# Two attentions in turn on one core: one more place for a piece before each first turn of maxima, and one load moved from a piece's place to the side of a unit

## The chip, the core and the metric

The kernel runs on one core of one Trainium2 chip. The time is the device time of one execution in microseconds (us), and lower is better. A core has a matrix engine (TensorE, PE in the profile; its weight loads are listed as PEld), a vector engine (VectorE, DVE), a scalar engine (ScalarE, ACT), a general engine (GpSimd, POOL) and an engine that only issues transfers (SyncE, SP). Each engine works through its own queue of instructions in order; they wait for one another through semaphores. Matrix products land in PSUM, which has eight banks of 128 partitions x 512 float32; the other engines read them from there. TensorE's clock can be cut; the profile gives the granted share.

## What is computed

Four batch elements of 1024 tokens with 256 channels go through two layers, each an attention and a feed-forward part, every one with a residual and a LayerNorm behind it:

```python
x = _layernorm(x + _L0_attn_ref(x, ...))  # 16 heads of 16; q and k normalised, rotated; softmax over all 1024 keys
x = _layernorm(x + _L0_ffn_ref(x, ...))   # silu(x Wg) * (x Wu), then Wd; hidden size 768
x = _layernorm(x + _L1_attn_ref(x, ...))  # 8 heads of 32, causal, with a geometric term in the scores
x = _layernorm(x + _L1_ffn_ref(x, ...))   # 16 experts, two per token, 12 of them MLPs of 1024
```

The change concerns the order of work around the second attention of each element (causal), which is in short

```python
scores = q @ k.T * scale, masked above the diagonal, + head_scales * geo
attn = softmax(scores)
out = (attn @ v) @ w_out
```

and the loading of the first attention's queries and keys of element 2.

## The kernel before

**Order by hand.** The program writes out the order of every engine's instructions itself (no scheduler moves them). The long stages are Python generators that emit a *unit* of attention work and then `yield`; `weave` (L1182) runs such a generator and emits *pieces* of other work between its units: projections, transposes and feed-forward parts of the same or the neighbouring element. After unit u of n it brings the number of emitted pieces up to `total * (u + 1) // n`. So the pieces are spread evenly over the units. Before the pieces of a unit, `tick()` emits the small steps that were booked for this point with `later(k, ...)` (k units later), and one entry of `side` is emitted from unit `side_at` on. Entries of `mid` are counted as pieces: from unit `at` on each takes the place of a unit's pieces.

**The stages.** First attentions and second attentions alternate: `first_units(1)`, then `second_units(0)` with element 1's pieces, then `first_units(2)`, `second_units(1)` and so on. The last second attention, `second_units(3)`, is run by a loop of its own with a plan of 29 entries.

**The first attention** (`first_units`, L1089, 64 units per element). A unit has four heads' scores (L491, `sc`), the maxima products of a coming group (L467, `mx`), the exponentials on ScalarE (L500, `pe`), the maxima on VectorE (L470) and the product with the values (L509, `av`). `load_heads(b, pr)` issues two transfers on SP (L379 and L380, `ss` and `xr`) and books eight small POOL steps (L386), one in each of the next eight ticks.

**The second attention** (`second_units(b)`, L1142, 29 units). Its first work is to find each row's maximum: `Maxima1.unit(t, u)` makes one block of scores for four heads (L972, `mx`, four banks), and VectorE reduces each bank (L982 with the mask on the diagonal, L986 without). There are 24 such blocks in four sets: (half 0, group 0) with four, (half 0, group 1) with four, and two sets of eight for half 1. After the last block of a set, `split` (L993 to L997) writes the maxima as three bfloat16 parts into `nm`, five small steps on VectorE in half 0. In the next unit, `turn` (L1002, `ptm`) transposes them on TensorE, and VectorE copies the result to `nmT` (L1005). The scores for the softmax (L1022, `sc`) take `nmT` as a second product, so that the maxima come off within PSUM; then exponentials (L1033), the mask on POOL (L1036), the product with the values and the sums (L1059, `av` and `dn`), and the division in four steps (L1077 on VectorE, L1079 on POOL).

How many blocks of maxima a unit has is written in `many`: one in units 0 to 3, two in unit 4, one in 5 to 8, two in 9 to 11, one in 12 to 19, none in the last nine. Scores begin when fewer than 19 blocks are left, that is in unit 5. So units 0 to 4 have only maxima. The first set ends in unit 3, and its turn is the first thing in unit 4.

**The pieces beside it.** For `second_units(0)` and `second_units(1)` there are 28: the nine of `first_end(b)`, numbered 0 to 8 here, are two transposes of the first attention's output (`pta`, L613), the last unload (`pto`, L524, L527, L528), two projections (`ppa`, L598, each with the residual and the LayerNorm's moments of two row tiles on VectorE, L553 to L556), two more `pta` and two more `ppa`; from 9 on come the first 19 of `ffn0(b)`: a transpose (`ptx`, L647), gate-and-up pieces (`gu`, L665, L675 to L678) and `down` pieces (`dn`, L683, each with a residual). For `second_units(2)` there are 45 pieces: the same nine and all 36 of `ffn0(3)`.

**Banks.** `ps_s` has six banks, given out in turn; a new user waits until the one six before it has been read. The blocks of maxima, the scores, `ptm` and all pieces in the second attentions take theirs from it. In the first attentions the pieces use the single bank of `ps_m`.

**The load in question.** In the weave of `first_units(1)`, `load_heads(2, 0)` is an entry of `mid` with `at` 30. The pieces there are 65: four of `project_v(1)`, nine of `first_end(0)`, 36 of `ffn0(0)` and 16 of `project1(0)`; numbers 30 and 31 are the two `down` pieces of the second quarter of `ffn0(0)`.

Of the kernel before, what the change touches and what calls it, by code (L numbers as in the profile page):

```python
# [20 lines left out]
B, S, C = 4, 1024, 256  # L21
# [14 lines left out]
def postln_layers_kernel(ctx: ExitStack, tc: tile.TileContext, a: dict, out: bass.AP):  # L36
# [75 lines left out]
    with ExitStack() as main:  # L112
# [27 lines left out]
        def bank(name, big):  # L140

            if big:
                return ps_s.tile([P, 512], F32, tag="s", name=name)
            return ps_m.tile([P, 512], F32, tag="m", name=name)
# [14 lines left out]
        def take_xin(b, j, name):  # L159
            key, t = xin_here.pop(0)  # L160
            assert key == (b, j, name)
            if xin_next and not xin_here:
                load_ahead()
            return t
# [127 lines left out]
        def project_v(b):  # L292
            def piece(j, big):
                xin = take_xin(b, j, "v") if b else xin0[j]
                ps = bank(f"v0_{b}_{j}", big)
                for i in range(2):
                    for c in range(2):
                        nc.tensor.matmul(
                            ps[:, i * 256 : (i + 1) * 256],
                            xin[:, c, i * P : (i + 1) * P],  # L300
                            w0[:, c, 512:768],
                            start=c == 0,
                            stop=c == 1,
                        )
                if b and xin_next:
                    load_ahead()
                nc.scalar.copy(va0[:, 2 * j : 2 * j + 2, :, 0:D0], ps.rearrange("p (t h d) -> p t h d", t=2, h=H0))

            return [lambda big, j=j: piece(j, big) for j in range(4)]
# [779 lines left out]
        def first_units(b):  # L1089

            oq0[b] = act.tile([P, TB, C], F32, tag="oq", bufs=2, name=f"oq0_{b}")
            last = None
            for g in range(G0):
                n = 4 * b + g
                at = Attend(groups[n], oq0[b])
                for i in range(16):

                    k, j = divmod(16 * n + i + LEAD, 16)
                    mx = groups.get(k)
                    for hp in range(2):  # L1100

                        then = []
                        for h in range(2):
                            if mx is not None:
                                then += [at.head(i, 2 * hp + h), mx.head(j, 2 * (1 - hp) + h)]
                            elif hp == 0:
                                then += [at.head(i, 2 * h), at.head(i, 2 * h + 1)]
                        for fn in then:
                            fn()
                        if hp == 0:  # L1110
                            if i > 0:
                                at.values(i - 1)
                            elif last is not None:
                                last.values(15)
                            if j == 3:
                                groups[k - 1].turn(0, 1, name="a")
                            if i == 5 and last is not None:
                                last.unload(1)
                            if j == 10 and mx is not None:
                                mx.turn(0, 0, name="a")  # L1120
                            if i == 11:
                                at.unload(0)
                            if j >= 12 and k + 1 in groups:
                                groups[k + 1].turn((j - 12) // 2, j % 2)
                    if j == 0:
                        groups[k - 1].close(1)
                    if j == 3 and k + 1 < G0 * B:
                        groups[k + 1] = Maxima(*divmod(k + 1, G0))
                    if j >= 4 and k + 1 in groups:
                        groups[k + 1].rotate(4)  # L1130
                    if j == 8 and mx is not None:
                        mx.close(0)
                    yield
                last = at
            last.values(15)

            def end(big):
                last.unload(1, big)

            ends[b] = end  # L1140

        def second_units(b):  # L1142


            oT1[b] = act.tile([P, G1, S], F32, tag="oq", bufs=2, name=f"oT1_{b}")
            mx = [Maxima1(b, g) for g in range(G1)]
            at = [Attend1(m, oT1[b]) for m in mx]
            halves = ([(t, 0) for t in range(4)], [(t, u) for t in range(4, TB) for u in range(2)])
            blocks = [(h, g) for h in range(2) for g in range(G1)]
            ahead = [(h, g, k) for h, g in blocks for k in range(len(halves[h]))]  # L1150
            scores = [(g, i) for h, g in blocks for i in ((0, 1, 2, 3) if h == 0 else range(4, 12))]
            many = [1] * 4 + [2] + [1] * 4 + [2] * 3 + [1] * 8 + [0] * 9
            last, to_turn = None, []
            for n in many:
                sc = scores.pop(0) if len(ahead) < 19 else None
                turns, to_turn = to_turn, []
                todo = [ahead.pop(0) for _ in range(n)]

                def maxima():
                    h, g, k = todo.pop(0)  # L1160
                    mx[g].unit(*halves[h][k])
                    if k == len(halves[h]) - 1:
                        mx[g].split(h)
                        to_turn.append((g, h))

                if sc is not None:
                    g, i = sc
                    at[g].scores(i)
                    if len(todo) > 1:
                        maxima()  # L1170
                if last is not None:
                    at[last[0]].values(last[1])
                last = sc
                for g, h in turns:
                    mx[g].turn(h)
                while todo:
                    maxima()
                yield
            assert not scores
            at[last[0]].values(last[1])  # L1180

        def weave(units, n, pieces, big, mid=(), at=0, side=(), side_at=0, rate=1):  # L1182


            mid, side = list(mid), list(side)
            done, total = 0, len(pieces) + len(mid)
            for u, _ in enumerate(units):
                tick()
                for _ in range(rate if u >= side_at else 0):
                    if side:  # L1190
                        side.pop(0)()
                if u >= at and mid:
                    mid.pop(0)(big)
                    done += 1
                    continue
                left = len(pieces)
                while left and (done < total * (u + 1) // n):
                    pieces.pop(0)(big)
                    done, left = done + 1, left - 1
            for piece in pieces:  # L1200
                piece(big)
                tick()
            for step in side:
                step()
                tick()
# [136 lines left out]
        def first_end(b):  # L1342

            out = out_project0(b)
            return out[:2] + [lambda big: ends[b](big)] + out[2:]
# [14 lines left out]
        load_heads(1, 1)  # L1360
        for t in range(TB):
            load_x(1, t)
        weave(first_units(1), 64, project_v(1) + first_end(0) + ffn0(0) + project1(0), False, [lambda big: load_heads(2, 0)], 30)
        for b in (1, 2):
            ffn = ffn0(b)
            weave(
                second_units(b - 1),
                29,
                first_end(b) + ffn[:cut],
                True,  # L1370
                side=load_v(b + 1) + [lambda b=b: load_heads(b + 1, 1)],
            )
            weave(
                first_units(b + 1),
                64,
                second_end(b - 1, ffn[cut:]) + project1(b),
                False,
                [lambda big, b=b: load_heads(b + 2, 0)] if b + 2 < B else (),
                30,
                dispatch(b - 1, False),  # L1380
                26,
            )
# [16 lines left out]
        nc.sync.dma_start(b1.rearrange("p e f -> p (e f)"), a["b1"])  # L1399
        b2 = mw.tile([P, EM, C], F32, name="b2")  # L1400
        nc.sync.dma_start(b2.rearrange("p e c -> p (e c)"), a["b2"].partition_broadcast(P))
        weave(second_units(2), 29, first_end(3) + ffn0(3), True)
        out2, (tu2, lo2) = out_project1(2), route(2)
        proj, out3, (tu, lo) = project1(3), out_project1(3), route(3)
        straight(proj[:4] + out2[:1] + proj[4:8] + out2[1:2])
# [350 lines left out]
```

## Time and profile before

| | |
|---|---|
| median of the runs | 2390.05 us (3 runs: 2387.06, 2390.05, 2404.72) |
| the profiled execution | 2392.53 us, of it the span from the first to the last instruction 2390.8 us |
| TensorE's granted clock, mean | 0.966 |
| first attention of element 1 (`first_units(1)`) | ends at about 693 us |
| first turns of the second attentions (L1002) | 705.56, 1173.38, 1629.55 and 1835.50 us |
| TensorE idle before them | 3.53, 3.05, 3.24 and 3.36 us |

A line of the profile's timeline gives the start, the duration, the engine, the line of the program, the operation, the tiles as out<-in, the shapes and the number of instructions merged; in square brackets stands the idle time of that engine before it and what ended it. A float32 product is two matmul instructions. A line of the waits gives who waited for whom, the total in us, the number of times and the longest. A window's line gives for each engine the busy time and the number of instructions. A busy TensorE isn't always at its peak: matmuls that wait for a bank between two others of the same line can be merged into one busy row.

### The profile page before, as it was taken

The page shows a single profiled execution, that of the slowest core. Times are in us where ns is not written, and L with a number is a line of the kernel's source. Part 1 is how long each engine was busy: PE and PEld are TensorE (multiplying, and loading weights), DVE is VectorE, ACT ScalarE, POOL GpSimd, SP SyncE. Part 2 cuts the span into 40 slices and gives each one's busy share as a digit, 9 for nine tenths or more (in the row PEclk, how much of TensorE's full clock was granted, in tenths as well). Part 3 has the DMA queues.
Part 4 walks back from the last instruction along what each step waited for, and adds up shares of the span by engine and source line. Part 5 has one row for each costly group of instructions (what it writes and reads, how often), then busy time and mean ns, then how long its engine had stood idle before and what let it go on. Part 6 is the DMA issues. An engine that isn't in the chain of part 4 may idle for free.

```text
span 2390.8 us, 36349 instructions
## 1 busy us (share of the span) xinstructions
PE 2287.3 (96%) x14004; PEld 1122.2 (47%) x14004; DVE 1384.3 (58%) x3259; ACT 1030.9 (43%) x2063; POOL 761.9 (32%) x1181
## 2 busy tenths in 40 slices
PE   8999999999999999999999999999999994999986
PEld 5333334444444444334444434345556443666654
DVE  7666666666557567776674767726645785111124
ACT  2665655554542355555324565562332331222222
POOL 5326337052105121553241321111112154222235
PEclk9999999999999999999899999998999986999998
DMA  4143121000000000000100000012000012444463
GB/s 112 52 149 117 60 75 35 1 28 1 1 28 1 1 1 1 28 28 28 55 1 1 1 1 8 31 34 103 1 1 1 1 55 71 107 122 108 107 181 95
DMA packets 81662, 109.63 MB, mean 46 GB/s; under 512 B 9040, under 2 KB 71248, under 8 KB 79824
## 3 DMA queue, kind: packets, MB, share of 16 engines
q1 hardware_dynamic: 52208, 73.87, 9.4%
q0 software_dynamic: 10176, 16.39, 3.4%
q10 hardware_dynamic: 19104, 17.04, 2.3%
q8 instruction: 110, 1.80, 0.3%
q14 instruction: 64, 0.52, 0.1%
HBM read 67.86 MB, written 39.42 MB: 45 GB/s over the span
## 4 chain that ended last, share of the span: by engine, by line
PE 86%; DVE 8%; DMA 2%; issue 1%; ACT 1%; POOL 1%; SPq 0%; DVEq 0%; POOLq 0%; ACTq 0%
PE sc L491 21%; PE av L509 10%; PE gu L665 7%; PE ph L1619 6%; PE py L1655 6%; PE mx L972 5%; PE sc L1022 4%; PE p L941 4%; PE dn L683 3%; PE av L1059 3%; PE ppa L598 3%; PE dn L1059 2%; PE mx L467 2%; DVE masked L982 2%; PE qk L321 2%; PE pt L458 1%
## 5 line engine op out<-in xcount | busy, mean ns | idle before, releaser
L470 DVE TENSOR_REDUCE part<-mx 128x1 f32<-128x512 f32 x1024 | 657.0, 684 | 311.1 <-PE mx L467 307.3
L500 ACT ACTIVATE pe<-sc 128x512 f32<-128x512 f32 x1024 | 554.7, 596 | 415.0 <-PE mx L467 388.0
L467 PE MATMUL mx<-kT,qT 32*128 32x512 f32 x2048 | 604.3, 639 | 0.6 <-DVE part L470 0.2
L491 PE MATMUL sc<-qT,kT 32*128 32x512 f32 x2048 | 586.2, 639 | 0.4 <-ACT pe L500 0.4
L509 PE MATMUL av<-pe,va 128*32 128x512 f32 x2048 | 273.0, 605 | 0.0
L491 PEld LDWEIGHTS sc<-qT,kT 32*128 32x128 f32 x2048 | 164.9, 183 | 212.4 <-issue 173.0
L1033 ACT ACTIVATE pe<-sc 128x512 f32<-128x512 f32 (+3 forms) x384 | 157.2, 497 | 203.5 <-PE sc L1022 203.4
L982 DVE CUSTOM_DVE_ANT_0 masked<-mx,mask_w 128x128 bf16<-128x128 f32 (+3 forms) x256 | 125.6, 491 | 111.6 <-PE mx L972 82.5
L1655 PE MATMUL py<-f,hTm 128*128 128x256 f32 x768 | 175.1, 387 | 14.6 <-DVE yo L1657 14.6
L467 PEld LDWEIGHTS mx<-kT,qT 32*128 32x128 f32 x2048 | 173.6, 183 | 18.7 <-DVE part L470 10.8
L1619 PE MATMUL ph<-dmT,f 128*128 128x512 f32 x384 | 168.6, 597 | 0.0
L1655 PEld LDWEIGHTS py<-f,hTm 128*128 128x128 f32 x768 | 148.5, 195 | 41.2 <-DVE yo L1657 15.4
L1657 DVE TENSOR_TENSOR yo<-py,b 128x256 f32<-128x256 f32 x48 | 20.3, 423 | 245.2 <-PE py L1655 245.2
L1036 POOL TENSOR_SCALAR_AFFINE_SELECT pe<-pe 128x256 f32<-128x256 f32 x128 | 52.0, 415 | 292.0 <-ACT pe L1033 290.4
L972 PE MATMUL mx<-kT,qT 32*128 32x512 f32 (+3 forms) x768 | 136.5, 569 | 3.6 <-DVE x L553 2.8
L386 POOL TENSOR_TENSOR ss<-ss,neg_half 128x16 f32<-128x16 f32 x48 | 139.1, 2911 | 0.6
L1663 POOL DMA_INDIRECT acc_d<-yo,dm x40 | 62.6, 1565 | 228.5 <-DVE yo L1660 180.2
L509 PEld LDWEIGHTS av<-pe,va 128*32 128x32 f32 x2048 | 40.4, 108 | 192.6 <-issue 188.7
L1022 PE MATMUL sc<-qT,kT 32*128 32x512 f32 (+3 forms) x768 | 122.7, 563 | 3.9 <-DVE part L982 1.6
L1627 ACT ACTIVATE hTm<-ph,b 128x512 f32<-128x512 f32 x96 | 60.7, 683 | 144.2 <-PE ph L1619 144.2
L1619 PEld LDWEIGHTS ph<-dmT,f 128*128 128x128 f32 x384 | 73.5, 192 | 88.0 <-issue 86.5
L665 PE MATMUL gu<-xTf,wg 128*128 128x256 f32 x384 | 110.2, 410 | 3.8 <-DVE hT L678 3.3
(370 smaller groups left out, 3013.1 us busy)
## 6 DMA issues: line engine op xcount, KB each, us to landing
f<-in_fc SPq DMA_DIRECT2D x14, 1024.0 KB, 4.9
f<-in_fc ACTq DMA_DIRECT2D x10, 1024.0 KB, 5.8
disp_d<-empty ACTq DMA_DIRECT2D x12, 520.0 KB, 3.4
xink<-in_xT SPq DMA_DIRECT2D x24, 256.0 KB, 3.0
qk_d<-xs SPq DMA_DIRECT2D x6, 1024.0 KB, 5.1
xr<-qk_d SPq DMA_DIRECT2D x6, 1024.0 KB, 5.9
dm<-disp_d SPq DMA_DIRECT2D x11, 520.0 KB, 5.7
x<-in_x SPq DMA_DIRECT2D x32, 128.0 KB, 2.5
```

Of the source, the lines that this page charges most:

```text
L467: nc.tensor.matmul(sc, self.qT[r, t * P : (t + 1) * P], self.kT[r, u * 512 : (u + 1) * 512], start=True, stop=True)
L470: return lambda: nc.vector.tensor_reduce(self.part[:, t, u, h : h + 1], sc, AX.X, ALU.max, negate=True)
L491: nc.tensor.matmul(sc, self.m.kT[r, kt * P : (kt + 1) * P], self.m.qT[r, qb * 512 : (qb + 1) * 512], start=True, stop=True)
L500: nc.scalar.activation(self.pes[i, h // 2][:, h % 2, :], sc, AF.Exp)
L509: nc.tensor.matmul(self.av[32 * h : 32 * h + 32, :], va0[:, kt, 4 * self.g + h, :], self.pes[i, h // 2][:, h % 2, :], start=kt == 0, stop= ...
L665: nc.tensor.matmul(ps[:, i * 256 : (i + 1) * 256], (wg, wu)[i][:, c, f * P : (f + 1) * P], xT[j][:, c, :], start=c == 0, stop=c == 1,)
L972: nc.tensor.matmul(scs[h][:, :n], qT[r, t * P : (t + 1) * P], kT[r, u * 512 : u * 512 + n], start=True, stop=True,)
L982: nc.vector.tensor_tensor_reduce(masked[:, :n], scs[h][:, :n], mask_w[:, 512 - n :], -1.0, -NEG, ALU.add, ALU.min, part)
L1022: nc.tensor.matmul(scs[h][:, off:], ones_h[r, :] if w else kT[r, kt * P : (kt + 1) * P], (self.m.nmT if w else qT)[r, q], start=w == 0, st ...
L1033: nc.scalar.activation(pe[:, j, off:], scs[2 * hp + j][:, off:], AF.Exp)
L1619: nc.tensor.matmul(ph[:, i * CAP : (i + 1) * CAP], f1[:, c, (f + i) * P : (f + i + 1) * P], dmT[:, c, :], start=c == 0, stop=c == 1,)
L1655: nc.tensor.matmul(py[:, :C], hT[:, f, c * P : (c + 1) * P], f2[:, f, :], start=f == 0, stop=f == FF1 // P - 1)
```

## The change

Two edits. In `second_units`, one more `yield` is put ahead of a turn, where a set of maxima has just been split, no scores have begun, and the element isn't the last. That is so once per element, in unit 4, for the elements 0, 1 and 2. At this `yield` the weave runs a tick, a side step if there is one, and the pieces that are due; the three weaves count 30 places instead of 29. In the weave of `first_units(1)`, `load_heads(2, 0)` goes from `mid` to `side`, from the same unit 30 on: it no longer counts as a piece and no longer takes the place of one.

```diff
@@ second_units
                         mx[g].split(h)
                         to_turn.append((g, h))
 
+                if turns and sc is None and b < B - 1:
+
+                    yield
                 if sc is not None:
                     g, i = sc
                     at[g].scores(i)
@@ the weaves
-        weave(first_units(1), 64, project_v(1) + first_end(0) + ffn0(0) + project1(0), False, [lambda big: load_heads(2, 0)], 30)
+        weave(
+            first_units(1),
+            64,
+            project_v(1) + first_end(0) + ffn0(0) + project1(0),
+            False,
+            side=[lambda: load_heads(2, 0)],
+            side_at=30,
+        )
         for b in (1, 2):
             ffn = ffn0(b)
             weave(
                 second_units(b - 1),
-                29,
+                30,
                 first_end(b) + ffn[:cut],
...
-        weave(second_units(2), 29, first_end(3) + ffn0(3), True)
+        weave(second_units(2), 30, first_end(3) + ffn0(3), True)
```

## The prediction

> **What bounds the kernel now.** I read the page's busy times first, then the waits, then the timeline and the table of stretches around the two edited places. All times are of the profiled execution: span 2390.8 us, 2392.53 us by the clock of the runs, so 1.7 us lie outside the span. That is 2.5 us above the median of 2390.05; 1% of the median is 23.9 us, which is about what a measurement of this kernel can tell from no change.
>
> ```profile
> PE 2287.3 (96%) x14004; PEld 1122.2 (47%) x14004; DVE 1384.3 (58%) x3259; ACT 1030.9 (43%) x2063; POOL 761.9 (32%) x1181
> PE 86%; DVE 8%; DMA 2%; issue 1%; ACT 1%; POOL 1%; SPq 0%; DVEq 0%; POOLq 0%; ACTq 0%
> ```
>
> TensorE (PE) carries 86% of the chain that ended last; VectorE (DVE) carries 8%. So a change of order can only win where PE stands idle, is held by a full buffer, or runs at a lower clock. The waits say where an earlier piece could help:
>
> ```profile
> PEld L1002 <- DVE nm L995: 25.2, 15, 3.8
> PE ptm L1002 <- DVE nm L995: 18.0, 11, 3.5
> ```
>
> L1002 turns the split maxima. It waits for L995, the last step of the split: 18.0 us of PE idle time over 11 waits, the longest 3.5. Four of these are the first turns of the four second attentions (3.53, 3.05, 3.24 and 3.36 us). The change touches the first three of them. The first, in time:
>
> ```profile
> 703.66 0.69 DVE L982 CUSTOM_DVE_ANT_0 masked<-mx,mask_w 128x512 bf16<-128x512 f32 x1
> ...
> 705.30 0.20 DVE L995 CAST nm<-part 128x16 bf16<-128x16 f32 x1
> ...
> 705.56 0.61 PE L1002 MATMUL ptm<-ident_h,nm 128*128 128x128 bf16 x4 [3.53 <-DVE nm L995]
> 706.10 2.85 PE L972 MATMUL mx<-kT,qT 32*128 32x128 f32 x16
> 708.88 3.78 PE L598 MATMUL ppa<-w0p,oTa 128*128 128x256 f32 x8
> 712.59 1.96 PE L1022 MATMUL sc<-qT,kT 32*128 32x512 f32 x8
> ```
>
> PE ends `pto` at 702.0 and waits; DVE works through four maxima and five small split steps without a gap. Then comes the first projection `ppa`, in 3.78 us; the next, at 716.83, takes 1.99. The table of stretches says why (columns: stretch, length, busy and count per engine, granted clock, DMA share and GB/s):
>
> ```profile
> 702.00:706.00 4.00, 0.47 (x5) 0.35 (x4) 3.50 (x13) 0.00 (x0) 0.00 (x0) 0.76 0.83 310
> 706.00:713.00 7.00, 7.00 (x30) 4.96 (x32) 3.76 (x19) 0.00 (x0) 0.00 (x0) 0.50 0.01 2
> 1170.00:1174.00 4.00, 0.95 (x10) 0.42 (x8) 3.42 (x13) 0.00 (x0) 0.00 (x0) 0.50 0.93 314
> 1630.00:1647.00 17.00, 17.00 (x62) 10.88 (x64) 10.14 (x41) 2.65 (x5) 1.74 (x4) 0.53 0.19 81
> ```
>
> After the wait PE has half its clock: for 7 us in the first attention, most of 17 in the third. In the second it has half of it already in the wait. The other edited place is element 1's first attention:
>
> ```profile
> 514.32 2.86 PE L683 MATMUL dn<-wd,hT 128*128 128x256 f32 x12
> 517.70 2.86 PE L683 MATMUL dn<-wd,hT 128*128 128x256 f32 x12 [0.52 <-DVE x L553]
> ```
>
> Two `down` pieces stand back to back, and the second waits for the one `ps_m` bank that the first filled.
>
> **The change part by part.**
>
> *Loading beside a unit.* As `mid`, the load took unit 30's place, so unit 30 had no piece and unit 31 two. As `side`, it issues the same two DMAs on SP and books the same eight POOL steps at the same tick; 65 pieces over 64 units then give one each until the last unit. Nothing on SP or POOL moves; the transfer has landed 5 us after issue and its cover (33 units) is unchanged. What goes is the 0.52 us wait, and the stretched first half of unit 31: its eight matmuls last from 510.27 to 512.25, where an unhindered half (513.25 to 514.32) takes 1.07; a weight load in it waited 0.71 for ACT. 1.98 - 1.07 + 0.52 = **1.4 us off**. At least the 0.5 goes.
>
> *The extra place, first and second attention.* 28 pieces over 30 places instead of 29: pieces 3 to 12 each come one unit earlier, unit 14 has none, and from unit 15 on all is as before. Piece 3, the first `ppa`, falls into the wait: 2.0 us at full clock in a 3.5 us hole. But its residual (two adds, two statistics, two aggregates: 712.70 to 714.79 on DVE, 2.06 us) now stands ahead of `nmT` and the next eight maxima on DVE, the busy engine here. PE's next eight matmul groups need banks that these free: the two of t=1 wait for the residual and for `nmT` (to 708.6), then for two maxima at 0.44. I get the next `ppa` at about 710.0 where one starts now at 708.88: 1.1 later. At half clock it ends 3.75 later, 713.8 against 712.59 now: 1.2 behind, with a 1.93 us piece more done: **0.8 off**; at full clock 2.6 off. In the second attention the same sum gives **0.9**. I take half clock for both, because the stretch from the turn to 707.4 has little work for PE.
>
> *The pieces one unit earlier.* Units 9 to 11 have two maxima each and DVE is nearly full there. `ppa` number four with its 2.06 us residual leaves unit 9 for unit 8, which has one; gate-and-up pieces (0.85 us on DVE) come in. DVE then starts unit 10's maxima about 1.9 us earlier (744.57 now). From 748.4 to 760.2 unit 11 takes 11.8 us, with the clock at half from 751.8 to 758.7. Were that dip gone, I count 8.9 us. Between 0.5 and 3.4, I take **2.0 for each of the two attentions**: near the DVE figure, since the dip is not sure to go. Unit 14 without a piece: a unit's 4.7 us of own matmuls hide 2.1 us of exponentials, so nothing; if that cover fails, 0.9, as in unit 31 above. The loads of the next heads issue at the same point of SP's queue; their POOL steps come one unit earlier, while POOL is idle (53 us before 716.0).
>
> *The third attention.* 45 pieces over 30. Into the hole comes only a `pta` (0.66 us); the two `ppa` that now run at half clock from 1640.25 to 1646.86 come a unit earlier, at 1633.6, back to back. That is PE's densest work, and in all three attentions the clock came back after such a stretch (ends 714.3, 1181.9, 1646.1). I expect it back near 1639, the next scores at 1644.1 instead of 1646.79, and 0.6 of work done ahead: **3.3 off**; at least 1, at most 4.5.
>
> Sum: 1.4 + 0.8 + 0.9 + 2 x 2.0 + 3.3 = 10.4; 2392.5 - 10.4 = 2382. By the lower ends it is 0.5 + 0 + 0 + 2 x 0.5 + 1 = 2.5 (2390); by the upper ends 1.4 + 2 x 2.6 + 2 x 3.4 + 4.5 = 17.9 (2374.6).
>
> **The rivals.**
>
> *The vector engine gives it all back* (slower). The chain from 698 to 705 is DVE's, and what is put ahead of its next maxima pushes them by 2.06 us. If the first scores follow DVE's last maximum instead of PE's `ppa`, each of three attentions pays the 2.06 and unit 14 its 0.9: 3 x 2.96 - 1.4 = 7.5, so 2400. It decides where PE is done before DVE; against it, DVE idles 1.82 us before the first residual today, so PE ends last by that much. In the third attention the piece has no residual, which weakens it again.
>
> *The gap was no loss.* The pieces fill it, the waits return at the banks, and only the edit on the load is won: -1.4, 2391. For it: both engines do the same work in the stretch, and DVE binds until 710.9.
>
> *The clock is held.* If the filled gap keeps the clock up, the 10.2, 17.1 and 17.1 us at half speed (from 704.0, 1164.8 and 1629.1) are in question. In them PE works without a long wait for 8.2 us (from 706.1), 8.5 (from 1173.4) and 11.4 (from 1634.7), 28 in all, of which full clock would save half; 2 of that are in the 3.3 already. So up to 12 beyond the forecast: 2370. Against it: in the second attention the clock fell at 1164.8, more than 5 us before the wait, in a stretch with no idle gap of TensorE. The Trainium skill ("TensorE: Matmul & The Clock Gate", HAM oscillation) would have it that idle gaps over some 3 us drop the clock to half and that shorter ones don't; by it, all three holes cut below 3 us would give this rival. The trace agrees with the half (0.50), but 1164.8 shows a fall without such a gap.
>
> *It doesn't do what it says.* The condition holds once per attention (unit 4: 20 tiles left, the split just made), and the places are then 30 in all three, as the callers say; I give this nothing.
>
> **How the numbers follow.** Forecast (5 to 17 off): 0.62, at **2382**. No loss in the gap: 0.18. Clock held: 0.10. Slower by DVE: 0.10. The range takes in the forecast's bounds, the 3 us that the lowest run lies under the median, and the no-loss rival: 2371 to 2395. It leaves out part of the slower and of the clock rival. None of the cases reaches 1% of 2390 by its own price (2366 or 2414), so: faster by over 1% 0.03, within 1% 0.95, slower by over 1% 0.02.
>
> **What would show it.** Right: `ptm`'s first wait falls from 3.5 to about 1.5 us in two attentions and by 0.6 in the third; `ppa` stands ahead of it; the 0.52 between the two `dn` is gone; unit 10's maxima start earlier against unit 9's; the third attention's half clock ends some 7 us sooner. Wrong: DVE ending the wait ahead of the first scores; a new idle gap at unit 14; a half-clock stretch longer than before. The sum is off if the clock falls or returns one window sooner or later: it decides most of the 2.0s and the 3.3.

## The result and the profile after

The changed kernel takes 2381.73 us (median of 17 runs, 2376.80 to 2386.51) where the kernel before takes 2390.05 (17 runs, 2385.08 to 2404.72). The ratio is 0.9955, with a 95% interval from 0.9942 to 0.9967; the two medians alone are 8.3 us apart (0.9965). The forecast was 2382, faster by less than 1%.

The profiled execution of after has a span of 2384.8 us. The chain and the waits that answer to those of before:

```profile
PE 85%; DVE 9%; DMA 2%; issue 1%; ACT 1%; POOL 1%; SPq 0%; DVEq 0%; POOLq 0%; ACTq 0%
```

```profile
PEld L1002 <- DVE nm L995: 21.7, 14, 3.6
PE ptm L1002 <- DVE nm L995: 14.6, 11, 3.4
```

TensorE waits 3.4 us less in sum for the split (18.0 before). That is far less than the 8.3 us won, so the shorter waits alone don't account for the result. The timeline of after around the first turn of the first second attention, with TensorE's rows and one of VectorE:

```profile
704.19 0.66 PE L524 MATMUL pto<-ident,avs 128*128 128x128 f32 x4
704.69 1.89 PE L598 MATMUL ppa<-w0p,oTa 128*128 128x256 f32 x8
...
708.42 0.40 PE L1002 MATMUL ptm<-ident_h,nm 128*128 128x128 bf16 x4 [1.84 <-DVE nm L995]
...
708.87 0.41 DVE L553 TENSOR_TENSOR x<-ppa,x 128x256 f32<-128x256 f32 x1
...
710.33 2.85 PE L972 MATMUL mx<-kT,qT 32*128 32x256 f32 x8 [0.46 <-DVE x L553]
...
713.11 3.23 PE L598 MATMUL ppa<-w0p,oTa 128*128 128x256 f32 x8
...
716.26 1.14 PE L1022 MATMUL sc<-qT,kT 32*128 32x512 f32 x8
```

The first `ppa` stands in the wait and takes 1.89 us; 1.84 us of waiting are left. Its residual is ahead of the next maxima on VectorE, and the products of the second block wait for it (0.46 us). The second `ppa` takes 3.23 us, partly at half clock. From the turn to the first scores it is 7.84 us, where it was 7.03: longer, as forecast, with one projection more done.

The clock is where the two profiles differ most. TensorE's granted clock in the second attentions of elements 0 to 3 (columns: stretch, length, busy time and count of PE, PEld, DVE, ACT and POOL, granted clock, DMA share and GB/s), first before, then after:

```profile
693.68:853.06 159.38, 151.49 (x1092) 76.20 (x1089) 92.80 (x269) 53.67 (x126) 46.39 (x63) 0.94 0.04 11
1160.57:1320.77 160.20, 152.80 (x1092) 76.80 (x1088) 92.81 (x269) 53.77 (x126) 47.06 (x64) 0.91 0.06 17
1615.53:1816.95 201.42, 193.94 (x1313) 115.53 (x1309) 114.51 (x324) 62.38 (x149) 29.74 (x70) 0.96 0.09 31
1816.95:2017.98 201.03, 161.97 (x1102) 85.07 (x1101) 145.21 (x485) 55.37 (x130) 72.28 (x155) 0.83 0.10 33
```

```profile
696.50:850.02 153.52, 147.25 (x1093) 74.98 (x1089) 91.96 (x269) 53.90 (x126) 46.63 (x63) 0.98 0.04 12
1157.58:1314.09 156.51, 149.58 (x1093) 74.83 (x1089) 92.13 (x269) 54.00 (x126) 47.29 (x64) 0.97 0.06 18
1608.90:1805.74 196.84, 187.52 (x1312) 111.35 (x1309) 114.15 (x324) 62.64 (x149) 29.88 (x70) 0.98 0.09 32
1805.74:2011.97 206.23, 167.57 (x1101) 87.22 (x1100) 145.24 (x485) 55.50 (x130) 72.17 (x155) 0.81 0.09 32
```

The three changed attentions take 506.9 us instead of 521.0, and the clock in them is 0.97 to 0.98 instead of 0.91 to 0.96. By the trace's record of the clock they stand at half clock for 23.9 us instead of 64.9. This pair is the widest apart: two later traces with these units as before give 514.4 and 515.2 us, four with them as in the change 507.2 to 509.8. The fourth, whose code is the same, took 5 us longer, at 0.81 instead of 0.83; and the first attention of element 0, also the same, 296.1 instead of 292.4. So one pair of profiles differs by several us in places that the change doesn't touch, and the experiments had to be read by stages and by the clock.

### The profile page after: what moved, and what is told of

It reads as the page before. It is cut to its first block, busy times and chain, and to the rows that moved or that the text cites. A ratio compares the mean times of both kernels' runs of the same rounds, so it can differ in the third digit from the quotient of the medians.

```text
span 2384.8 us, 36347 instructions
## 1 busy us (share of the span) xinstructions
PE 2281.3 (96%) x14004; PEld 1117.3 (47%) x14004; DVE 1381.8 (58%) x3259; ACT 1033.2 (43%) x2063; POOL 763.5 (32%) x1181
## 4 chain that ended last, share of the span: by engine, by line
PE 85%; DVE 9%; DMA 2%; issue 1%; ACT 1%; POOL 1%; SPq 0%; DVEq 0%; POOLq 0%; ACTq 0%
PE sc L491 21%; PE av L509 10%; PE gu L665 7%; PE ph L1629 6%; PE py L1665 6%; PE mx L972 4%; PE sc L1022 4%; PE p L941 4%; PE dn L683 3%; PE av L1059 3%; PE ppa L598 2%; PE mx L467 2%; PE dn L1059 2%; DVE masked L982 2%; PE qk L321 2%; PE pt L458 1%
```

## The experiments

All runs but those of the result were made in three groups, each on one chip and beside the kernel before. Two quantities are worked out for each: the sum of the three changed second attentions in its profiled execution, with the time at half clock in it, and, from all its runs, the half-clock time of the whole execution, 2 x (1 - granted clock) x span. The ratios are those on record; they are near the quotients of the medians, but not the same.

| kernel | median us (runs) | ratio to before, 95% interval | half clock, mean us | attentions 0 to 2: us / of it at half clock |
|---|---|---|---|---|
| before, by group | 2389.4 (35), 2393.0 (35), 2393.8 (28) | | 153, 162, 162 | 521.0 / 64.9 |
| before, again | 2396.2 (12) | 1.0004 (0.9985 to 1.0023) | 164 | 514.4 / 47.8 |
| the change; again | 2381.7 (17); 2383.9 (11) | 0.9955 (0.9942 to 0.9967); 0.9949 (0.9932 to 0.9965) | 127; 131 | 506.9 / 23.9; 507.2 / 23.9 |
| load edit only | 2390.3 (12) | 1.0003 (0.9981 to 1.0025) | 162 | 515.2 / 51.2 |
| extra place only | 2382.3 (12) | 0.9972 (0.9956 to 0.9987) | 127 | 509.0 / 37.5 |
| place behind the turn | 2388.0 (12) | 0.9984 (0.9967 to 1.0000) | 141 | 517.4 / 47.8 |
| hole behind unit 4 | 2387.9 (12) | 1.0001 (0.9978 to 1.0023) | 151 | 521.8 / 61.4 |
| hole behind unit 5 | 2387.3 (12) | 0.9971 (0.9954 to 0.9987) | 146 | 508.2 / 34.1 |
| unread products in the wait | 2390.3 (12) | 0.9982 (0.9951 to 1.0012) | 139 | 508.9 / 27.3 |
| hole behind unit 4, filled with unread products | 2401.4 (12) | 1.0016 (0.9992 to 1.0040) | 155 | 520.4 / 47.8 |
| the change and unread products | 2384.0 (12) | 0.9950 (0.9926 to 0.9973) | 121 | 511.5 / 27.3 |
| a place in the fourth too; again | 2379.4 (12); 2379.4 (6) | 0.9941 (0.9917 to 0.9965); 0.9938 (0.9915 to 0.9961) | 127; 124 | 507.6 / 34.1; 509.8 / 34.1 |

**The two edits apart.** The first kernel has the load as `side` and everything else as before; the second has the extra place, and the load as `mid`.

```diff
# load edit only, against before
-        weave(first_units(1), 64, ..., False, [lambda big: load_heads(2, 0)], 30)
+        weave(first_units(1), 64, ..., False, side=[lambda: load_heads(2, 0)], side_at=30)
# extra place only, against the change
-            side=[lambda: load_heads(2, 0)],
-            side_at=30,
+            [lambda big: load_heads(2, 0)], 30
```

> Edit on the load alone, second attentions as before. My theory: 1.4 us off, all of it in units 30 to 32 of element 1's first attention (18.4 us instead of 19.8), so about 2388.6 against 2390; the first turns' waits stay at 3.0 to 3.5 us. Rival (the load was most of the win): 5 us or more off.

> The extra place alone, the load as before. My theory: about 7 us off (8.3 less 1.4), 2383; units 30 to 32 of element 1's first attention take 19.8 us again; first waits 1.8, 1.8 and 2.8 us as in the changed kernel. Rival (the load was most of the win): 3 us off or less.

From the start of unit 30 to that of unit 33, element 1's first attention takes 19.80 us in the traces with `mid` and 18.36 in all with `side`. So the load edit is worth 1.44 us; its runs can't show so little (0.9981 to 1.0025). The extra place alone has 0.9972, and the two intervals overlap with that of the change: the place is nearly all of the win. The rival that the load was most of it is out. One expectation missed: the first two waits with the extra place alone are 0.91 and 0.00 us in its trace instead of 1.8. The projections in them ran for the most part at half clock and took 2.57 and 3.03 us, where the changed kernel's took 1.89.

**The wait filled, or the pieces earlier?** One kernel moves the extra place behind the turn: all pieces come as early as in the change, only the wait stays empty. The other leaves unit 4 without a piece: the first projection stands in the wait and every other piece where it stood before.

```diff
# place behind the turn, against the change
-                if turns and sc is None and b < B - 1:
-                    yield
...
                 for g, h in turns:
                     mx[g].turn(h)
+                if turns and last is None and b < B - 1:
+                    yield
# hole behind unit 4, against the change (extra=4; the weaves count 29)
-                while left and (done < total * (u + 1) // n):
+                while left and (done < total * (u + 1 - (u > extra)) // n):
```

> Both edits, but the extra place stands behind the turn instead of ahead of it: the pieces come as early in the later units as in the change, the waits aren't filled. Theory A (filling the wait is what pays in units 3 to 6, about 1.9 us in each of two attentions, and the earlier pieces about 3 us more in units 9 to 15): waits of 3.0 to 3.5 us stay, about 3 us of the 8.3 are lost, 2385. Theory B (the earlier pieces alone pay): 2382, same as the change within 2 us. Theory C (the filled wait alone pays): 2388 or more.

> Both edits, but the place behind unit 4 stays empty, so that only the piece in the wait comes earlier and all others stand where they stood before. Theory A: waits of 1.8, 1.8 and 2.8 us, units 9 to 15 as long as before, about 4 us of the 8.3 lost, 2386. Theory B (the earlier pieces alone pay): 2388 or more. Theory C (the filled wait alone pays): 2382.

Neither half won what the change wins. The runs with the place behind the turn lie at 0.9984, on the edge of the load edit's own 0.9994; those with the hole at 1.0001. The intervals are wide and leave room for theory A, whose 2385 and 2386 are a ratio of about 0.998. The traces say more. The three attentions take 161.1, 158.4 and 197.9 us with the place behind the turn, and 160.6, 159.8 and 201.4 us with the hole; in three traces with these units as before they take 157.4 to 159.4, 154.1 to 160.2 and 201.2 to 201.4. So the filled wait alone won nothing in its trace, and the earlier pieces alone won only in the third attention.

The third attention is the clearest place. Two projections that stand behind the first scores in the kernel before stand ahead of them in the change. Before, then after:

```profile
1640.25 6.61 PE L598 MATMUL ppa<-w0p,oTa 128*128 128x256 f32 x16
1646.79 0.93 PE L1022 MATMUL sc<-qT,kT 32*128 32x384 f32 x8
```

```profile
1627.64 5.07 PE L598 MATMUL ppa<-w0p,oTa 128*128 128x256 f32 x16
1632.64 1.14 PE L1022 MATMUL sc<-qT,kT 32*128 32x512 f32 x8
```

In all eight traces that have the pair ahead of the first scores this attention takes 196.7 to 198.3 us, with 6.8 to 10.2 of it at half clock, also where its wait isn't filled. In five of the six that have the pair behind them it takes 201.2 to 202.5 us, with 13.7 to 17.1 at half clock. The sixth, with unread products in the wait (below), takes 198.9 us with 6.8.

In the first attention the hole's trace shows how the filled wait is given back. The first scores start 3.99 us after the turn instead of 7.03, yet units 5 and 6 then take 20.5 us instead of 14.9:

```profile
706.91 0.40 PE L1002 MATMUL ptm<-ident_h,nm 128*128 128x128 bf16 x4 [0.73 <-DVE nm L995]
...
710.90 2.81 PE L1022 MATMUL sc<-qT,kT 32*128 32x512 f32 x6
...
717.38 3.78 PE L598 MATMUL ppa<-w0p,oTa 128*128 128x256 f32 x8
...
721.10 1.40 PE L1022 MATMUL sc<-qT,kT 32*128 32x384 f32 x8
```

```profile
707.00:711.90 4.90, 3.84 (x24) 2.40 (x24) 4.13 (x18) 0.00 (x0) 3.23 (x3) 1.00 0.04 17
711.90:722.10 10.20, 10.17 (x35) 6.33 (x36) 5.06 (x18) 2.06 (x4) 3.68 (x3) 0.50 0.00 0
```

The scores stretch to 2.8 us: their weight loads wait three times for maxima that VectorE has not read yet (0.15, 0.15 and 0.28 us), and while TensorE does so little, the clock falls to half for three windows of 3.4 us. The next projection runs at half clock again. That is the slower rival's place, though not its price: VectorE's maxima come last there.

**Is it the clock?** Unread products keep TensorE busy and move nothing. In the first kernel six of them stand in the wait of the kernel before; in the second four fill the hole of the last experiment; in the third three follow the piece in the changed kernel's wait.

```diff
+        def spin(name, n):
+            w = ps_m.tile([P, 512], F32, tag="m", name=f"spin_{name}")
+            for _ in range(n):
+                nc.tensor.matmul(w[:, 0:256], ones, wd[:, 0, :], start=True, stop=True)
# in the wait: 6 in the kernel before, 3 in the changed one; in the hole: 4, at the end of unit 4
+                if turns and sc is None and b < B - 1:
+                    spin(f"w{b}", 6)
                 for g, h in turns:
                     mx[g].turn(h)
```

> The kernel before, with six products whose result nobody reads (2.9 us at full clock) put ahead of the first turn in elements 0 to 2: TensorE works through the wait, no piece moves and VectorE gets nothing. Theory K (what pays is that the clock is at half for less time): the clock falls one or two windows of 3.4 us later but still falls, since the stretch behind the turn has little work; it is back after the first projection as before, so 3 to 10 us less at half clock per attention, 0.4 us of time for each: 4 to 8 us off, 2382 to 2386. Theory P (moving useful work into the wait is what pays): no gain, 2389 to 2391.

> The kernel with the piece in the wait and an empty place behind unit 4, with four such unread products (1.9 us at full clock) in that empty place. Theory K: the empty place cost the clock; dense products there bring it back by the time of the first scores or one window later, the half-clock stretches fall from about 10 to 7 us, and the time falls from 2388 to 2384 or 2385, though 2 us of idle products per attention are added. Theory P: the products only cost, 2390 to 2394.

> The change, with three unread products (1.4 us at full clock) behind the piece in the wait, ahead of the first turn of elements 0 to 2. Theory K: the clock still falls in the stretch behind the turn; 0 to 3 us off, 2379 to 2382. Theory P: nothing, 2382, since what is left of the wait (1.8, 1.8 and 2.8 us) covers them.

In the first one's trace these are the same units as in the prediction's first timeline, with no piece moved:

```profile
701.98 2.75 PE L1145 MATMUL spin_w<-wd,ones 128*128 128x256 f32 x12
705.67 0.40 PE L1002 MATMUL ptm<-ident_h,nm 128*128 128x128 bf16 x4 [0.94 <-DVE nm L995]
706.00 2.01 PE L972 MATMUL mx<-kT,qT 32*128 32x128 f32 x16
707.94 1.99 PE L598 MATMUL ppa<-w0p,oTa 128*128 128x256 f32 x8
709.87 1.19 PE L1022 MATMUL sc<-qT,kT 32*128 32x512 f32 x8
```

The turn comes no earlier (705.67 against 705.56), but the `ppa` behind it takes 1.99 us instead of 3.78, and the scores start 2.7 us sooner, because the clock stayed up through these units. In that execution the three attentions took 508.9 us, almost as little as with the change. So in one execution keeping the clock was enough to win as much. The runs don't show that it is so each time. They fall into two groups of six, 2378.5 to 2383.1 us at a granted clock of 0.973 to 0.977 and 2397.4 to 2399.4 at 0.965 to 0.967, with none near the median; the traced execution is of the first. What the slow six lost is not on record, and it need not be in the changed units: the fourth second attention takes 201.0 to 207.1 us in nine of the twelve traces that have it unchanged, and 214.2 to 215.2 in three.

The second kernel missed both expectations: half clock in the three attentions fell from 61.4 to 47.8 us, as theory K had it, but their time only from 521.8 to 520.4, and the runs show no gain (1.0016). Its trace is also one of the three with a long fourth attention (214.2 us), so its median isn't the price of the products alone. The third won nothing on the change: 0.9950.

**The dense piece behind unit 4.** The empty place is moved one unit on: the first projection in the wait, the second behind unit 4, none behind unit 5, the rest as before (`extra=5`).

> Both edits, with the empty place behind unit 5: the first projection stands in the wait and the second behind unit 4, all later pieces where they stood before. Empty place behind unit 4: 2388, nothing won; empty place behind unit 14: the change, 2382. Theory K (a dense piece behind unit 4 brings the clock back, and the later units matter only through their own dips): units 3 to 6 as in the change, units 9 to 15 as before; the second attentions 0 to 2 take about 512 us together, between 518 before and 507 to 509 with the change: 2384 to 2386. Theory L (the shift in units 9 to 15 is what pays): 2388 or more.

Up to the turn of unit 7 this kernel has done the same pieces as the one with the hole behind unit 4, and as the kernel before. Those units of the first attention take 37.4 us with the hole behind unit 4, 33.8 to 34.6 in three traces of before's order, and 31.0 here. (Five traces of the change's order take 31.8 to 35.5 us for them, with a transpose of 0.66 us more done, so one trace of each kernel is thin evidence.) In this trace the clock was at half from 698.6 to 705.4, nearly as in the other one (698.2 to 705.0), so the two came to the turn alike; then:

```profile
706.36 0.40 PE L1002 MATMUL ptm<-ident_h,nm 128*128 128x128 bf16 x4
...
710.53 1.99 PE L598 MATMUL ppa<-w0p,oTa 128*128 128x256 f32 x8
712.46 1.19 PE L1022 MATMUL sc<-qT,kT 32*128 32x512 f32 x8
```

With a projection at 710.5 the clock stays up until 749.8; with nothing there it fell at 711.9 for 10.2 us. The three attentions take 508.2 us, close to the change's 507. By this trace theory L is out for the attentions themselves. The time, 2387.3, lies between the two ends and above the expected 2386; its interval overlaps with the change's, and its fourth attention was long in the trace (215.0 us). Whether the shift of the later pieces is worth the rest is not settled.

**The change and the kernel before once more.**

> The change once more, on the chip of the others: 2380 to 2384; the second attentions 0 to 2 take 505 to 511 us together, at 20 to 40 us of half clock.

> The kernel before, for another trace: the second attentions 0 to 2 take 514 to 522 us together, at 50 to 65 us of half clock, where the change's take 505 to 511 at 20 to 40. If they take less than 512, the two traces of before in hand were unlucky ones.

The change came as expected. The kernel before took 2396.2 us, the three attentions within their range at 514.4 us, but with 47.8 us at half clock where at least 50 were expected. The fourth attention of this trace of before took 215.2 us, that of the other 201.0, with the same program:

```profile
1810.22:2025.43 215.21, 175.39 (x1102) 90.05 (x1101) 145.14 (x485) 55.38 (x130) 71.47 (x155) 0.76 0.09 31
```

**A place in the fourth attention too.** The condition `b < B - 1` is dropped, and one of unit 4's two projection pieces in the hand-written plan goes to the new place.

```diff
-                if turns and sc is None and b < B - 1:
+                if turns and sc is None:
...
+        plan.insert(4, [plan[4].pop(0)])
         for u, _ in enumerate(second_units(3)):
```

> The change, with an extra place ahead of the first turn in the fourth second attention too: one projection piece of unit 4's two (2.0 us, no VectorE work) goes into its wait of 3.36 us. All theories: the wait there falls to about 1.4 us; 1.5 to 3 us off against the change, 2379 to 2380. If it gives nothing, the bank or VectorE's maxima were what unit 4 waited for.

> The change with a place ahead of the fourth first turn as well, beside the change itself: 2 to 3 us less than the change (wait of 3.4 us to about 1.4), 2378 to 2380.

In the second of these groups the six runs lie from 2374.4 to 2379.8 and the change's eleven from 2379.2 to 2387.9; the medians differ by 4.5 us. The fourth attention's first turn:

```profile
1818.21 1.99 PE L941 MATMUL p<-xTa,w1q 128*128 128x256 f32 x8 [0.29 <-ACT xTa L648]
1821.28 0.40 PE L1002 MATMUL ptm<-ident_h,nm 128*128 128x128 bf16 x4 [1.07 <-DVE nm L995]
...
1823.54 3.66 PE L941 MATMUL p<-xTa,w1k 128*128 128x256 f32 x8
```

The wait of 3.36 us is down to 1.07, and the piece there needs nothing of VectorE. This version beats both kernels: 2379.4 in two groups, 0.994 of before. Its fourth attention takes 198.3 and 196.3 us where the change's two traces have 206.2 and 207.1, which is more than the wait gave; the time at half clock in it is 64.6 and 61.0 us instead of 77.8 and 78.5. That the place caused this too is not shown.

## Why the prediction was right, and where its steps were off

The sum was 10.4 us off, from 2392.5 to 2382; measured were 8.3 by the medians of the same group. That the time itself was met to 0.3 us is partly luck: the sum was taken off a profiled execution that lay 2.5 us above the median, and off the median it would have given about 2380. By stages, with the three traces in which these units run as in the kernel before (the load edit's among them) and the five in which they run as in the change (the extra place alone and the two with a place in the fourth attention among them), the extra place gave 516.9 - 508.1 = 8.8 us in the attentions, where the terms came to 9.0.

- **The load.** 1.4 forecast, 1.44 measured, in the place named.
- **The waits.** Forecast about 1.5, 1.5 and 0.6 less in the third; measured 1.84, 1.80 and 2.80 (0.44 less). The scores after the first turn were to start later with one projection more done: 7.84 us behind the turn against 7.03, as forecast.
- **The first, second and third attention.** Forecast 2.8, 2.9 and 3.3. Measured, as means over those traces: 4.1 (158.6 to 154.5), 0.4 (157.0 to 156.6) and 4.3 (201.3 to 197.1). The sum holds; the shares of the first two don't, though the kernel before itself takes from 154.1 to 160.2 us in the second.
- **The step that failed** is the reading of the first two attentions' sum as two terms that stand by themselves: a filled wait (0.8 and 0.9) and the pieces one unit earlier (2.0 each). Added up they nearly fit, 4.5 us against 5.7. Cut at the turn of unit 7, by which the change has done one transpose of 0.66 us more, the means even give the two terms: 1.8 and -0.5 for the early units, 2.2 and 1.0 for the later ones. But neither came alone. These two attentions together take 315.5 us before and 311.0 with the change, but 320.4 with the filled wait alone and 319.5 with the earlier pieces alone, in one trace of each.
- **What goes with the gain** is the clock: the three attentions stand at half clock for 30.7 us instead of 54.6. Over the fourteen traces their length follows that time, 498 us plus 0.37 us for each us at half clock, with a scatter of 2.2 us; the largest miss is 4.8, where unread products are added. Over the runs of single kernels the line is much the same, 0.26 to 0.42 us per us. Read at 140 us of half clock, the kernel before takes 2386.3 to 2388.0 us and the change 2386.3 and 2386.6. At equal clock they are within 2 us; in the group that has both, the change has 131 us of half clock instead of 162. All this is a correlation. That less half clock is the cause rests on three comparisons: the third attention with its pair of projections behind or ahead of the first scores, the unread products in the wait, which move no piece, and the hole behind unit 4 or 5. The last two rest on single traces, so for the first two attentions the cause is not fully shown.
- **The third attention's clock.** The two projections moved up, the half-clock stretch was to end 7 us sooner: it lasts 6.8 us instead of 17.1. Right in kind, 3.3 forecast against 4.3.
- **The hole at unit 14.** It was costed at nothing, with 0.9 if the cover fails. It failed, and not where it was looked for: with no piece ahead of them, unit 15's scores hardly wait for ScalarE's exponentials (0.22 us), but for the maxima just ahead of them, which VectorE has not read yet (0.75 and 0.31 us):

```profile
775.83 2.23 PE L1022 MATMUL sc<-qT,kT 32*128 32x512 f32 x7
776.77 0.29 PEld L1022 LDWEIGHTS sc<-qT,kT 32*128 32x128 f32 x2 [0.75 <-DVE part L986]
777.37 0.18 PEld L1022 LDWEIGHTS sc<-qT,kT 32*128 32x128 f32 x1 [0.31 <-DVE part L986]
```

They take 2.81 us (775.83 to 778.64 in the changed kernel) where they take 1.37 behind a piece. So 1.4 us are lost in each of two attentions, and the change still wins.
- **The rivals.** "The clock is held" had 0.10 and a price beyond the forecast. Less half clock is most of what happened, but not in the place that it named. Behind each first turn the clock still falls, for 6.8 us in the first trace of the change; on the means the early units of the first and second attention stand at half clock for 9.5 and 11.8 us instead of 14.8 and 11.4. The rest is the later dips (6.8 and 4.5 us down to 0.7 and 1.2) and the third attention (17.1 to 7.5), which the forecast had in its own terms. "VectorE gives it all back" is what the hole's trace shows in the first attention, at less than its price; "The gap was no loss" fits the runs of that same kernel.

## What to carry to other kernels

Ask of a filled wait not only how many us of idle time it takes away, but what TensorE does in the next few windows of some 3.4 us: if that is thin work that waits for another engine, the clock can fall and the gain be given back, and a dense piece right behind it can be worth more than the one in the wait. When a few us of effect are to be found, compare stages, and compare runs at the same granted clock: here the same program's runs differ by up to 23 us, along with the clock, more than twice the whole effect. A place that is taken from another unit has a price there: look for scores that then find their banks still full.

## What the runs showed of the hardware

- The half-clock stretches of all fourteen traces come in steps of 3.41 us (3.4, 6.8, 10.2, 13.7, 17.1 and more), but for the last of each trace, which its end cuts. The Trainium skill ("TensorE: Matmul & The Clock Gate", What's actually happening) gives a free-running window of 3413 ns; the traces agree with its length.
- The clock fell without long idle gaps. In the changed kernel it fell at 708.8, and in its second trace at 706.4, right behind waits of 1.84 and 1.85 us; at 1170.6 in the second trace 3.7 us after the wait had ended, with no gap over 0.77 us since; in the kernel before at 1164.8, ahead of the wait. The Trainium skill ("TensorE: Matmul & The Clock Gate", Why this matters for your kernels) warns of idle gaps over about 3 us; here short waits or thin work were enough.
- One unchanged stage, the fourth second attention with what follows it up to the experts, took 201.0, 201.2 and 215.2 us in three traces of the same code, at 65 to 103 us of half clock. What decides between these was not found.
